# Local attention: values and sums in 64-key by 32-column tiles over 192 of 256 queries, in two turns with scores and the q, k projection between

## The chip, the core and the metric

The kernel runs on one core of a Trainium2 chip. A core has five engines that work side by side[...]: TensorE (PE in the profile; its weight loads are shown apart as PEld), VectorE (DVE), ScalarE (ACT), GpSimd (POOL), and SyncE (SP), which here only issues DMAs. PE writes its results into PSUM, a memory of eight banks; DVE and ACT read them from there[...]. The metric is the device time of one run in microseconds (us), lower is better; the times given are medians.

## The reference, cut to what matters

Two residual layers follow each other: `x = x + latent_attention(layernorm(x))`, then `x = x + ffn(layernorm(x))`, on x of 8 x 1024 x 256 in fp32. The "ffn" is itself a small transformer of two layers with local attention, and it is this part that the change touches. In it, per layer, with windows of 128 tokens, 8 heads and 64 dimensions a head:

```python
qkv = h @ wqkv
q = l2norm(q) * qs
k = l2norm(k) * ksc
q, k = rotary_xpos(q, k)
...
sim = jnp.einsum('bhwid,bhwjd->bhwij', bq, bk)        # a window's queries, its own and the previous window's keys
mask = (i < j) | (i > j + WINDOW) | (j == -1)
attn = jax.nn.softmax(jnp.where(mask, -big, sim), axis=-1)
out = jnp.einsum('bhwij,bhwjd->bhwid', attn, bv)
x = x + o @ wo
...
x = x + (a * gelu(g)) @ w2 + b2                       # the layer's MLP
```

A query sees keys of its own window up to itself, and of the window before from its own position on. Over one block of 128 keys, own and next window together, a key is therefore seen by at most 129 queries out of 256.

## The kernel before, in words

The kernel has two stages. `mla` does the latent attention for all eight sequences; `local` does the two layers of local attention and MLP. The change is in `local` alone.

`local` goes through 16 passes, one for each layer and sequence, and each pass through 8 windows: 128 steps in all, and then 11 more to finish. All work of the four compute engines in this loop is in an order written out by hand (`tc.manual_schedule`, L1026): each engine carries out its instructions in the order in which the loop emits them, and no engine takes one out of turn. A step does not work on one window from start to end; it takes one piece of several windows, so that results are ready long before they are read. In step s the kernel before emits, in this order (L1038 to L1052):

- `qk` of window s (L763): PE projects q and k into a tile of two PSUM banks. ACT squares it (L774), DVE multiplies with cosines and sines (L776, L779) and sums the squares by head (L784, L785), POOL computes the reciprocal norms (`rn`, L125), adds the two rope products (L788) and multiplies by the norms (L789).
- `transposes` of window s-2 (L802): q and k are turned on PE, in four transposes each, and ACT copies them out of PSUM as `qT` and `kT`.
- `v` of window s (L792): the projection of the values, copied out by ACT.
- one unit of the MLP.
- `values` of window s-4 (L847): PE multiplies the probabilities with the values (o) and with a column of ones (s, the sums), for four heads at a time, each head in 32 columns of the array and all 128 keys in its rows. A window has two blocks of keys, the one before and its own; the first window of a pass has one. DVE then takes the reciprocal of s and multiplies o with it (L869 to L878).
- `scores` of window s-3 (L813): for each half of the heads, sixteen matmuls on tiles of 64 rows by 32 columns over 160 queries. The scores are for the keys of this window against the queries of this and the next one, so the `qT` of window s-2 is needed. ACT takes the exponential (L834) and POOL sets to zero what a query must not see, in two `affine_select` instructions (L836 for the own window, L841 for the next one). The results are `pts`, two tiles for each window, read by `values` in the next step and once more in the one after that.
- every second step `output` (L882), the projection with `wo`, added by DVE and sent to DRAM.
- a second unit of the MLP.

The MLP works on chunks of 512 tokens, and each chunk is eight units (`mlp`, L927): five units with two up-projections each (`ag`, L945; one for the gate, which ACT turns through Gelu, L953, and one which DVE multiplies with it, L954), one with the single leftover up-projection (L958 to L967), and two with the down-projection (`psy`, L978), of which the second also turns the next chunk (L710). With two units a step, four steps are one chunk. The steps that end or begin a pass also turn the input of the next one (L737).

The PSUM pools (L585 to L588) hold two tiles of two banks, "pair", which `qk` and the two halves of `scores` use in turn; three buffers of one bank, "mm", for everything else on PE; and one bank for o. The sums s stand in an "mm" buffer. ACT loads a table before an exponential if the last one was for Gelu, and the other way round; these loads are at L834, L953 and L961.

Of the kernel before, what the change touches and what calls it, by code (L numbers as in the profile page):

```python
# [29 lines left out]
F32 = mybir.dt.float32  # L30
AF = mybir.ActivationFunctionType
ALU = mybir.AluOpType
AX = mybir.AxisListType
PSUM = bass.MemoryType.PSUM

P = 128
# [20 lines left out]
DEPTH, HEADS, DH, WINDOW = 2, 8, 64, 128  # L57
# [24 lines left out]
def preln_mla_local_kernel(  # L82
# [27 lines left out]
    nc = tc.nc  # L110
# [5 lines left out]
    ident = const.tile([P, P], F32, name="ident")  # L116
    make_identity(nc, ident)
    half = const.tile([P, 16], F32, name="half")
# [458 lines left out]
    def local(ctx: ExitStack, verdict):  # L577
# [4 lines left out]
        p1 = ctx.enter_context(tc.tile_pool(name="l1", bufs=1))  # L582
# [3 lines left out]
        psum = ctx.enter_context(tc.tile_pool(name="psum3", bufs=3, space=PSUM))  # L586
        ppair.append(ctx.enter_context(tc.tile_pool(name="pair1", bufs=1, space=PSUM)))
        pacc = ctx.enter_context(tc.tile_pool(name="pacc3", bufs=1, space=PSUM))  # L588
# [12 lines left out]
        ys = [dram.tile([T + 1, D], F32, tag=f"y{i}", name=f"y{i}") for i in range(3)]  # L601
        zero = p1.tile([1, P], F32, name="zero")
# [145 lines left out]
        class Pass:  # L748
# [53 lines left out]
            def transposes(self, i):  # L802
                key = self.key(i)
                self.kTs[i] = p1.tile([P, 4, P], F32, tag="kT", name=f"kT{key}", bufs=2)
                r = self.rot.pop(i)
                for n, dst in ((0, qT[:, :, i * P : (i + 1) * P]), (1, self.kTs[i])):
                    ps = psum.tile([P, 4, P], F32, tag="mm", name=f"psq{key}_{n}")
                    flat = r[:, n].rearrange("p h d -> p (h d)")
                    for c in range(4):
                        nc.tensor.transpose(ps[:, c, :], flat[:, c * P : (c + 1) * P], ident)  # L810
                    evac(dst, ps)

            def scores(self, i):  # L813

                n = 2 if i + 1 < NT else 1
                kT = self.kTs.pop(i)
                self.pts[i] = []
                for g in range(2):
                    key = f"{self.key(i)}_{g}"


                    flat = next(turns)
                    for c in range(2):
                        for j in range(2):
                            rows = slice(64 * j, 64 * j + DH)
                            for t in range(4):
                                keys = slice(32 * t, 32 * t + 32)
                                q0, q1 = 32 * t, min(32 * t + 32 + P, n * P)
                                nc.tensor.matmul(  # L829
                                    flat[keys, 2 * j + c, q0:q1], kT[rows, 2 * g + c, keys],  # L830
                                    qT[rows, 2 * g + c, i * P + q0 : i * P + q1], start=True, stop=True,
                                )
                    pt = p1.tile([P, 4, 2 * P], F32, tag="pt", name=f"pt{key}", bufs=5)
                    nc.scalar.activation(pt[:, :, : n * P], flat[:, :, : n * P], AF.Exp, scale=-1.0)  # L834

                    nc.gpsimd.affine_select(  # L836
                        out=pt[:, :, :P], in_=pt[:, :, :P], pattern=[[0, 4], [1, P]],
                        compare_op=ALU.is_ge, fill=0.0, base=0, channel_multiplier=-1,
                    )
                    if n == 2:  # L840
                        nc.gpsimd.affine_select(  # L841
                            out=pt[:, :, P:], in_=pt[:, :, P:], pattern=[[0, 4], [-1, P]],
                            compare_op=ALU.is_ge, fill=0.0, base=0, channel_multiplier=1,
                        )
                    self.pts[i].append(pt)

            def values(self, i):  # L847

                key, vs, pts, oTs = self.key(i), self.vs, self.pts, self.oTs
                blocks = [(i - 1, P)] if i else []  # L850
                blocks.append((i, 0))
                o = pacc.tile([P, 2, 2, P], F32, tag="acc", name=f"o{key}")
                s = psum.tile([P, 2, P], F32, tag="mm", name=f"s{key}")
                for g in range(2):
                    for a in range(3):
                        for m, off in blocks:
                            for j in range(4):
                                h = 4 * g + j
                                rows = slice(32 * j, 32 * j + 32)
                                if a < 2:  # L860
                                    left = vs[m][:, h * DH + a * 32 : h * DH + a * 32 + 32]
                                nc.tensor.matmul(  # L862
                                    o[rows, g, a, :] if a < 2 else s[rows, g, :],
                                    left if a < 2 else ones,
                                    pts[m][g][:, 2 * (j % 2) + j // 2, off : off + P],
                                    start=(m == blocks[0][0]), stop=(m == i),
                                )
                rs = p2.tile([P, 2, P], F32, tag="lrs", name=f"rs{key}")
                nc.vector.reciprocal(rs, s)  # L869
                if i % 2 == 0:  # L870
                    oTs[i // 2] = p2.tile([P, 4, 2 * P], F32, tag="oT", name=f"oT{key}")
                at = self.n * NT + i
                nc.vector.tensor_reduce(stats[:, 1, at : at + 1], s, AX.XY, ALU.add)
                nc.vector.tensor_tensor(
                    oTs[i // 2][:, :, (i % 2) * P : (i % 2 + 1) * P].rearrange("p (g a) q -> p g a q", g=2),
                    o, rs.unsqueeze(2).to_broadcast([P, 2, 2, P]), ALU.mult,
                )
                nc.vector.tensor_reduce(stats[:, 0, at : at + 1], rs, AX.XY, ALU.add)  # L878
                if i:
                    del vs[i - 1], pts[i - 1]  # L880
# [26 lines left out]
        made = {}  # L907
# [111 lines left out]
        def each(step, name, back):  # L1019
            j = step - back  # L1020
            if 0 <= j < windows:
                n, i = divmod(j, NT)
                getattr(made[n], name)(i)

        E = mybir.EngineType
        with tc.manual_schedule(engines={E.PE, E.DVE, E.Activation, E.Pool}):  # L1026
            for step in range(windows + LAG):
# [9 lines left out]
                if not late:  # L1037
                    each(step, "qk", 0)  # L1038
                each(step, "transposes", 2)
                if not late:  # L1040
                    each(step, "v", 0)
                if step >= LAG:
                    next(units, None)
                each(step, "values", 4)
                each(step, "scores", 3)
# [5 lines left out]
                if step >= LAG - 2:  # L1051
                    next(units, None)  # L1052
                if late:
                    each(step, "qk", 0)
                    each(step, "v", 0)
# [621 lines left out]
```

## Time and profile before

| | |
|---|---|
| median of 3 runs | 3622.2 us (3621.33 to 3624.78) |
| the profiled execution's own time | 3623.07 us |
| its span, first to last instruction | 3621.2 us |
| mean granted PE clock | 0.995 |
| PE busy | 3556.6 us (98%) |
| DVE, ACT, POOL busy | 2246.5, 1828.0, 1348.9 us |
| `local`: first qk to the last step's qk | about 1061 to 3482 us |

The profile is one execution. "Busy" is the time in which an engine had at least one instruction running; PE's matmuls overlap, so that a mean of 274 ns for one says little of what it costs in a row of them. Each fp32 matmul of the program stands in the trace as two matmul records, with two weight loads. An arrow "<-" after an idle time names what ended it.

### The profile page before, as it was taken

How to read it: one execution, taken by the hardware profiler on the slowest of the kernel's cores; microseconds unless marked ns; L12 is line 12 of the kernel's file. 1: busy time of each engine (PE TensorE's matmuls, PEld its weight loads, DVE VectorE, ACT ScalarE, POOL GpSimd, SP SyncE). 2: the span in 40 equal slices, each digit the busy share in tenths (PEclk: the TensorE clock that was granted, in tenths of full speed). 3: DMA queues.
4: the chain of work that ended last, by engine and by line, in shares of the span. 5: the costliest groups of instructions: out<-in, count | busy, mean ns of one | idle time of the engine just before them, and what ended most of it. 6: DMA issues, size and time to landing. Idle time of an engine off the chain costs nothing.

```text
span 3621.2 us, 77779 instructions
## 1 busy us (share of the span) xinstructions
PE 3556.6 (98%) x34338; PEld 2046.6 (57%) x34338; DVE 2246.5 (62%) x3273; ACT 1828.0 (50%) x2362; POOL 1348.9 (37%) x1031
## 2 busy tenths in 40 slices
PE   8999999999999999999999999999999999999999
PEld 3434443443345666666666666666666666666666
DVE  6888888888876545555555554555555555555543
ACT  5777777777653344444444444444444444444441
POOL 1001000100118545545454553545455454444530
PEclk9999999999999999999999999999999999999999
DMA  1000000000110000000010001111101110110011
GB/s 58 7 19 24 16 12 21 24 7 7 69 56 13 19 33 19 31 27 31 22 37 30 19 31 57 36 33 45 45 25 36 33 36 26 43 42 24 26 33 42
DMA packets 102838, 110.14 MB, mean 30 GB/s; under 512 B 12930, under 2 KB 87003, under 8 KB 102363
## 3 DMA queue, kind: packets, MB, share of 16 engines
q1 hardware_dynamic: 99354, 101.49, 8.8%
q8 instruction: 271, 4.44, 0.5%
q10 hardware_dynamic: 3136, 3.59, 0.3%
q14 instruction: 77, 0.62, 0.1%
HBM read 63.11 MB, written 41.94 MB: 29 GB/s over the span
## 4 chain that ended last, share of the span: by engine, by line
PE 90%; DVE 5%; ACT 3%; issue 1%; DMA 1%; POOL 0%; ACTq 0%; SPq 0%; DVEq 0%; POOLq 0%
PE ag L945 14%; PE pair L769 12%; PE psy L978 9%; PE sc L399 9%; PE acc L432 7%; PE psw L890 6%; PE o L862 6%; PE pv L796 6%; PE psq L810 3%; PE s L862 3%; PE pair L829 3%; DVE rs L869 2%; PE psq L183 2%; PE psR L183 2%; ACT pt L834 2%; PE psx L183 1%
## 5 line engine op out<-in xcount | busy, mean ns | idle before, releaser
L125 POOL TENSOR_TENSOR rn<-ss,half 128x16 f32<-128x16 f32 x128 | 372.1, 2907 | 1028.8 <-DVE ss L785 1028.8
L421 DVE TENSOR_TENSOR pt<-pt,er 128x1024 f32<-128x1024 f32 x576 | 678.3, 1224 | 6.9 <-ACT pt L407 6.7
L407 ACT ACTIVATE pt<-sc 128x1024 f32<-128x1024 f32 x576 | 558.9, 1023 | 244.1 <-PE sc L399 220.0
L945 PE MATMUL ag<-d,l 128*128 128x512 f32 x1408 | 641.3, 597 | 3.4 <-ACT qT L78 2.7
L769 PE MATMUL pair<-l_qkv,xT 128*128 128x512 f32 x1024 | 466.9, 599 | 3.7 <-ACT pt L834 2.0
L834 ACT ACT_TABLE_LOAD x120 | 154.0, 1283 | 620.4 <-PE pair L829 620.3
L945 PEld LDWEIGHTS ag<-d,l 128*128 128x128 f32 x1408 | 262.0, 190 | 311.7 <-issue 303.2
L776 DVE TENSOR_TENSOR t<-pair,l_cos 128x1024 f32<-128x1024 f32 x128 | 156.5, 1223 | 354.7 <-ACT sq L774 354.7
L399 PE MATMUL sc<-q,k 32*128 32x512 f32 (+3 forms) x3072 | 350.9, 524 | 7.4 <-ACT pt L407 7.0
L769 PEld LDWEIGHTS pair<-l_qkv,xT 128*128 128x128 f32 x1024 | 189.7, 191 | 237.6 <-issue 206.5
L869 DVE RECIPROCAL rs<-s 128x256 f32<-128x256 f32 x128 | 224.6, 1755 | 157.8 <-PE s L862 157.7
L954 DVE SCALAR_TENSOR_TENSOR hid<-ag,l_b,ge 128x512 f32<-128x512 f32 x160 | 120.2, 751 | 317.6 <-ACT ge L953 178.4
L380 POOL TENSOR_SCALAR_AFFINE_SELECT er<-er 128x128 f32<-128x128 f32 x64 | 62.7, 980 | 678.5 <-DVE least L378 678.5
L432 PE MATMUL acc<-pt,v 128*32 128x512 f32 (+3 forms) x3072 | 312.0, 500 | 1.9 <-DVE pt L421 1.9
L788 POOL TENSOR_TENSOR t<-t,t 128x1024 f32<-128x1024 f32 x128 | 306.4, 2394 | 0.0
L978 PE MATMUL psy<-l,hid 128*128 128x256 f32 x1280 | 297.1, 379 | 0.0
L774 ACT ACTIVATE sq<-pair 128x1024 f32<-128x1024 f32 x128 | 131.1, 1024 | 313.0 <-issue 218.8
L978 PEld LDWEIGHTS psy<-l,hid 128*128 128x128 f32 x1280 | 243.2, 190 | 46.7 <-issue 15.3
L862 PE MATMUL o<-pt,v 128*32 128x128 f32 x7680 | 260.1, 274 | 0.8 <-POOL pt L836 0.8
L862 PEld LDWEIGHTS o<-pt,v 128*32 128x32 f32 x7680 | 204.2, 110 | 85.7 <-issue 82.8
L834 ACT ACTIVATE pt<-pair 128x1024 f32<-128x1024 f32 (+1 forms) x256 | 234.7, 968 | 34.6 <-PE pair L829 33.3
L399 PEld LDWEIGHTS sc<-q,k 32*128 32x128 f32 x3072 | 141.0, 184 | 189.8 <-ACT pt L407 113.6
(132 smaller groups left out, 5188.4 us busy)
## 6 DMA issues: line engine op xcount, KB each, us to landing
y<-xs SPq DMA_DIRECT2D x128, 128.0 KB, 1.9
h<-y SPq DMA_DIRECT2D x32, 512.0 KB, 3.8
x<-in_L_attn_x_dram SPq DMA_DIRECT2D x16, 512.0 KB, 4.6
x2d<-x SPq DMA_DIRECT2D x32, 256.0 KB, 2.3
xs<-x2d SPq DMA_DIRECT2D x16, 512.0 KB
x<-x2d SPq DMA_DIRECT2D x16, 512.0 KB
xs<-xs SPq DMA_DIRECT2D x32, 256.0 KB, 2.6
xs<-xs SPq DMA_DIRECT2D x16, 512.0 KB, 5.4
```

Of the source, the lines that this page charges most:

```text
L125: nc.gpsimd.tensor_tensor(out_, in_, half[:, :n], ALU.pow)
L399: nc.tensor.matmul(two[n // 2][:, n % 2, lo : lo + w], self.k[g][rows, kb * P : (kb + 1) * P], self.q[rows, g // 2, q0 : q0 + w], start=Tr ...
L407: nc.scalar.activation(pt, sc, AF.Exp, scale=SCALE)
L421: nc.vector.tensor_tensor(t, t, er.to_broadcast([P, 1024 // w, w]), ALU.mult)
L432: nc.tensor.matmul(self.acc[g][32 * n : 32 * n + 32, q0 - c * 512 :], self.v[:, kb, h * VW : h * VW + 32], pts[n // 2][:, n % 2, lo : lo + w],
L769: nc.tensor.matmul(qk[:, n].rearrange("p h d -> p (h d)"), self.left(i)[c], w["qkv"][:, c, n * INNER : (n + 1) * INNER], start=(c == 0), s ...
L788: nc.gpsimd.tensor_tensor(t1, t1, t2, ALU.add)
L834: nc.scalar.activation(pt[:, :, : n * P], flat[:, :, : n * P], AF.Exp, scale=-1.0)
L862: nc.tensor.matmul(o[rows, g, a, :] if a < 2 else s[rows, g, :], left if a < 2 else ones, pts[m][g][:, 2 * (j % 2) + j // 2, off : off + P ...
L869: nc.vector.reciprocal(rs, s)
L945: nc.tensor.matmul(ps, w["1"][:, c, i, :], d[:, c, :], start=(c == 0), stop=(c == 1))
L978: nc.tensor.matmul(ps[:, t, :], left, w["2"][:, i, :], start=(i == 0), stop=(i == NF))
```

## The change

It has five parts.

- **Tiles of values.** The keys of a block are cut in two halves of 64. A matmul of `values` now has 64 rows by 32 columns, so that eight instead of four run side by side, and each half of a block is only multiplied for the queries that can see it: 128 for one half and 64 for the other. The sums are one more part of the same tile, which grows to two banks; the two halves of rows write to different banks (`g = half ^ turn`).
- **Two turns.** In turn 0 the first half of keys does heads 0 to 3 and the second half heads 4 to 7; turn 1 is the other way round. After turn 1 comes the division.
- **Order of the step.** It is now: transposes of q, values turn 0, scores half 0, transposes of k, qk, scores half 1, values turn 1, v, a unit, output, a unit. In steps without qk a unit stands in its place, and near the end one unit moves ahead.
- **Buffers.** "mm" has two buffers instead of three.
- **Table switches.** A one-element Gelu follows scores half 1 on ACT, and a one-element exponential ends the step; each brings the load of its table to that place.

```diff
-        psum = ctx.enter_context(tc.tile_pool(name="psum3", bufs=3, space=PSUM))
+        psum = ctx.enter_context(tc.tile_pool(name="psum3", bufs=2, space=PSUM))
...
+        spot = p1.tile([1, 2], F32, name="spot")
+        nc.gpsimd.memset(spot, 0.0)
...
-            def values(self, i):
-                key, vs, pts, oTs = self.key(i), self.vs, self.pts, self.oTs
-                blocks = [(i - 1, P)] if i else []
-                blocks.append((i, 0))
-                o = pacc.tile([P, 2, 2, P], F32, tag="acc", name=f"o{key}")
-                s = psum.tile([P, 2, P], F32, tag="mm", name=f"s{key}")
-                for g in range(2):
-                    for a in range(3):
-                        for m, off in blocks:
-                            for j in range(4):
-                                h = 4 * g + j
-                                rows = slice(32 * j, 32 * j + 32)
-                                if a < 2:
-                                    left = vs[m][:, h * DH + a * 32 : h * DH + a * 32 + 32]
-                                nc.tensor.matmul(
-                                    o[rows, g, a, :] if a < 2 else s[rows, g, :],
-                                    left if a < 2 else ones,
-                                    pts[m][g][:, 2 * (j % 2) + j // 2, off : off + P],
-                                    start=(m == blocks[0][0]), stop=(m == i),
-                                )
+            def values(self, i, turn):
+                vs, pts = self.vs, self.pts
+                if turn == 0:
+                    self.o = pacc.tile([P, 2, 4, P], F32, tag="acc", name=f"o{self.key(i)}")
+                own = [(i, 0, 0, P), (i, 0, P // 2 if i else 0, P)]
+                before = [(i - 1, P, 0, P // 2), (i - 1, P, 0, P)]
+                blocks = [own[:1] + before[:1], before[1:] + own[1:]] if i else [own[:1], own[1:]]
+                last = len(blocks[0]) - 1
+                for a in range(3):
+                    for n in range(last + 1):
+                        for j in range(4):
+                            for half in range(2):
+                                m, off, q0, q1 = blocks[half][n]
+                                g = half ^ turn
+                                h = 4 * g + j
+                                keys = slice(64 * half, 64 * half + 64)
+                                left = vs[m][keys, h * DH + a * 32 :][:, :32] if a < 2 else ones[keys]
+                                nc.tensor.matmul(
+                                    self.o[32 * j : 32 * j + 32, g, a, q0:q1], left,
+                                    pts[m][g][keys, 2 * (j % 2) + j // 2, off + q0 : off + q1],
+                                    start=(turn == a == n == 0), stop=(turn == 1 and a == 2 and n == last),
+                                )
+                if turn == 1:
+                    self.divide(i)
...
-                if not late:
+                attend = step < windows and not late
+                end = windows + 2 <= step < windows + 4
+                each(step, "transposes", 2, 0)
+                each(step, "values", 4, 0)
+                each(step, "scores", 3, 0)
+                each(step, "transposes", 2, 1)
+                if attend:
                     each(step, "qk", 0)
-                each(step, "transposes", 2)
-                if not late:
+                else:
+                    for _ in range(1 + end):
+                        next(units, None)
+                each(step, "scores", 3, 1)
+                nc.scalar.activation(spot[:, 1:], spot[:, :1], AF.Gelu)
+                each(step, "values", 4, 1)
+                if attend:
                     each(step, "v", 0)
-                if step >= LAG:
-                    next(units, None)
-                each(step, "values", 4)
-                each(step, "scores", 3)
+                    if step >= LAG:
+                        next(units, None)
...
-                if step >= LAG - 2:
+                if step >= LAG - 2 and not end:
                     next(units, None)
+                nc.scalar.activation(spot[:, 1:], spot[:, :1], AF.Exp)
```

`transposes` and `scores` do what they did, now for one of their two halves at a call; `divide` holds the lines that ended `values`, with s read from the third part of o.

## The prediction

> **What bounds the kernel now.** I read the page first, for the busy shares, the forty slices and the costliest groups:
>
> ```profile
> PE 3556.6 (98%) x34338; PEld 2046.6 (57%) x34338; DVE 2246.5 (62%) x3273; ACT 1828.0 (50%) x2362; POOL 1348.9 (37%) x1031
> ...
> POOL 1001000100118545545454553545455454444530
> ...
> L862 PE MATMUL o<-pt,v 128*32 128x128 f32 x7680 | 260.1, 274 | 0.8 <-POOL pt L836 0.8
> ```
>
> PE is busy throughout; from slice 12 on (about 1060 us, where the local attention begins) POOL is at about half. The values' matmuls lose 0.8 us in all to POOL's masks: that wait is hidden today, and it is the one I follow. Next, the groups kept apart by shape, for 1300 to 3560 us: name, count, then busy us and mean ns.
>
> ```profile
> L862 PE MATMUL o<-pt,v 128*32 128x128 f32 x6912 | 233.6, 274 | 0.0
> ...
> L862 PE MATMUL s<-pt,ones_l 128*32 128x128 f32 x3456 | 136.5, 273 | 0.0
> L829 PE MATMUL pair<-qT,kT 64*32 64x160 f32 x6359 | 131.2, 299 | 0.0
> ```
>
> Values and sums take 370 us of PE in that stretch; a saving has to come from there. Then the timeline of one step (columns: start us, length us, engine, line, what):
>
> ```profile
> 2416.36 3.60 PE L769 MATMUL pair<-l_qkv,xT 128*128 128x512 f32 x8
> 2419.79 1.04 PE L810 MATMUL psq<-ident,t 128*128 128x128 f32 x8
> 2420.04 1.02 ACT L774 ACTIVATE sq<-pair 128x1024 f32<-128x1024 f32 x1 [3.17 <-issue]
> ...
> 2421.10 1.23 DVE L776 TENSOR_TENSOR t<-pair,l_cos 128x1024 f32<-128x1024 f32 x1 [3.44 <-ACT sq L774]
> ...
> 2424.68 0.17 DVE L785 TENSOR_SCALAR ss<-ss 128x16 f32<-128x16 f32 x1
> 2424.94 2.91 POOL L125 TENSOR_TENSOR rn<-ss,half 128x16 f32<-128x16 f32 x1 [10.98 <-DVE ss L785]
> 2425.91 1.08 PE L862 MATMUL o<-pt,v 128*32 128x128 f32 x32
> ...
> 2427.81 2.37 POOL L788 TENSOR_TENSOR t<-t,t 128x1024 f32<-128x1024 f32 x1
> ...
> 2428.67 1.32 PE L829 MATMUL pair<-qT,kT 64*32 64x160 f32 x64
> ...
> 2430.26 1.90 POOL L789 TENSOR_TENSOR t<-t,rn 128x1024 f32<-128x1024 f32 x1
> ...
> 2432.11 0.63 POOL L836 TENSOR_SCALAR_AFFINE_SELECT pt<-pt 128x512 f32<-128x512 f32 x1
> ```
>
> PE ends qk at 2419.79; POOL ends that window's rope multiply at 2432.16, 12.37 us later, and only then masks the scores. Across the steps this 12.37 is the median and nearly the minimum. It costs nothing now: the masks' reader, values, comes in the next step, at about 2443.4. Last, busy time by stretch (PE, then the other engines), on the grid on which the granted clock changes (PEclk, third number from the end):
>
> ```profile
> 1074.53:1077.94 3.41, 1.35 (x7) 0.53 (x7) 2.47 (x4) 0.00 (x0) 2.77 (x2) 1.00 0.00 0
> 1077.94:1081.36 3.42, 3.42 (x10) 1.87 (x9) 1.35 (x2) 1.99 (x3) 3.22 (x2) 0.50 0.00 0
> ```
>
> A stretch of 3.41 us with PE mostly idle is followed by one at half clock.
>
> **The skill.** TensorE: Matmul & The Clock Gate, section "Architectural detail": the queues of ScalarE, VectorE and GpSimd are strict FIFO. The trace agrees: a mask never passes the rope multiply ahead of it. The same page, Part 1: the clock is halved after an idle window of about 3.4 us; the two rows above agree. TensorEngine Tiling (Array Packing), "Key Properties": tiles work independently, and changing the mode drains the array. The trace agrees: the eight 64x32 tiles of scores start 7 ns apart and every eight take 0.136 us (160 columns); the four 128x32 tiles of values take 0.109 us (128 columns); around each change of mode about 0.09 us is empty.
>
> **The saving.** Now a window with two blocks has 96 records, 24 fours x 0.109 = 2.62 us. After it, a turn has for each of three parts two eights of 128 columns and two of 64: 3 x (2 x 0.109 + 2 x 0.055) = 0.98 us, both turns 1.97. No 64-column eight is in the trace; 0.055 is half of 0.109 and also eight starts of 7 ns. At worst it costs the full 0.109 (2.62, nothing saved). I take 0.055: 0.65 us saved per window, nothing in the first window of each pass (no block before). Mode changes go from three to four a step: +0.09. Net -0.56 us where PE sets the pace; 16 passes x (7 x 0.65 - 8 x 0.09) = 61 us at most.
>
> **The moved mask.** A step is now: q transposes, values turn 0, scores half 0, k transposes, qk, scores half 1, values turn 1, v, units. POOL's order, as built, is: masks of half 0, rn, add, multiply (all of this step's qk), masks of half 1. The next step's values turn 0 reads half 1 after its first eights (0.22 us), and everything on PE queues behind it: scores, transposes, the next qk. From the end of qk to that mask's end: 12.37 + 0.64 = 13.0 us, with PE's wake of 0.05 (its start after a mask at 1124.39). PE's work in that time: mode change 0.09, half the scores 0.54, values 0.98, change 0.09, v 1.72, units U, transposes 0.44, change 0.09, first eights 0.22: 4.2 + U. From release to the next qk's end: 0.76 + 0.54 + 0.09 + 0.44 + 3.43 = 5.26. So no step is shorter than 13.0 + 5.26 = 18.27 us. An up unit is 3.43. U is 6.9 in a step with two (A), 10.3 with an output too (B), 5.1 with one and the leftover chunk (C), over 14 with two down units (D). A lacks 1.9, C 3.7 us; B and D are covered.
>
> **The table switches and the third buffer.** The Exp dummy sits after the last unit; the next ACT item is the q copy, for which scores half 0 wait. The switch is 1.28 us (row of L834 loads). In A and C the mask is later still, so this is free; without the mask C would pay some 1.5. In D it is paid: with two buffers in place of three the chunk's second group of transposes waits for the adding of psy (0.2 + 0.69 + 0.05, less the 0.44 of the first group): +0.5; then evacuation 0.77, switch 1.28, dummy (not in the trace, 0.1 to 0.3; 0.2 taken), copy 0.58: scores start 1.55 late. Together 2.05 us. In the D of a pass that also turns the next stream, the same waits push its transposes: 2.75. The two switches each step replace those at L834 and L953; ACT at 50% hides them elsewhere. One memset: nothing.
>
> **Sum.** Qk to qk, the steps of a pass now repeat as D 24.81, A 17.10, B 19.24, C 15.61, D 26.11, A 19.02, B 20.55, C 15.61 = 158.05 us, 14 times from 1241.6 to 3482 us (one odd step at the layer change, left as it is). After: 26.3, 18.27, 19.0, 18.27, 28.3, 18.27, 20.0, 18.27 = 166.7: +8.65, x14 = 121. The three steps before: +2.6. The seven steps from the first scores to the first chunk's units (1081.8 to 1169.9 us: 88.1 us, 12.6 each) have little PE work and become 7 x 18.27 = 127.9: +39.8. Together +163. The clock: in C PE now idles 3.4 us on end, and in this trace every stretch of the grid with at most 1.54 us of PE busy was followed by half clock (six before the end), those with 1.73 and 1.82 were not; by where the grid falls that is about 8 cases in 10, each losing half of most of a 3.41 us window in the path to the next qk: 1.2 x 29 = 35; the seven idle steps at the start 10. Both from 0 to twice that. Tail and the join to the first stage: 0, +-5. 3621.2 + 208 = 3829 span; around it lie 1.9 us (3623.07), and the median 3622.2 stands 0.9 under that run. Forecast 3830 us.
>
> **Rivals.** *The clock holds.* The mask binds, but the half clock is not granted, as gaps are broken by small matmuls: 3622 + 163 = 3785. For it: the price rests on six stretches of this trace. *The mask is hidden (faster).* If the masks of half 1 are ready within 9.3 us of qk's end, PE's work in C, nothing waits and the tiles' 61 us are gained: 3561; with D's waits of 4.8 us a pass still there, about 3630. Against: 12.37 us is the sum of seven measured instructions on queues that keep order. The turning point is 9.3 us for C and 11.0 for A. *The halves don't overlap.* If the two row halves run one after the other, a turn costs 1.97: +0.8 in A and C, +2 in B and D, some 165 us more: 3990. Against: scores run so already. *It cancels:* 3622.
>
> **Chances.** Mask and clock 0.55, mask alone 0.26, mask hidden and faster 0.07, D's waits alone (3630, just slower) 0.04, no overlap 0.05, cancels 0.03. A difference under 0.2% (7 us) can't be told here. Faster 0.07, same 0.04, slower 0.89. The range holds the two mask cases with their unknowns: 3740 (163 less 45) to 3890 (clock at twice its price, 0.3 us more per wait).
>
> **What would show it.** PE's values waiting for POOL's mask, about 1.9 us in A and 3.7 in C, POOL never idle between the multiply and that mask; steps of 18.3 us or more in place of 15.6; scores waiting for the q copy after D; granted clock under 0.99; PE's busy share near 92%. Wrong if masks of half 1 start before the multiply ends, or if C stays under 17 us.

## The result, and the profile after

The changed kernel takes 3906.7 us (median of 4 runs, 3903.89 to 3908.08) against 3623.4 us before: ratio 1.0782, 95% interval 1.0765 to 1.0799. It is slower by 283 us, where I had forecast 208 slower; 3906.7 lies 17 us above the upper end of my range. The profiled execution has a span of 3905.2 us against 3621.2, and a mean granted clock of 0.977 against 0.995.

The page of the kernel after: busy time by engine, POOL and the granted clock in forty slices, and the costliest group of the new matmuls (busy us, mean ns | idle of PE ahead of them, and what ended it).

```profile
PE 3643.8 (93%) x45858; PEld 2096.4 (54%) x45858; DVE 2223.0 (57%) x3273; ACT 1947.5 (50%) x2683; POOL 1355.2 (35%) x1032
...
POOL 1000100010154544445444544444444444444440
PEclk9999999999978999999999999999999999999999
...
L876 PE MATMUL o<-pt,v 64*32 64x128 f32 (+1 forms) x15360 | 274.4, 254 | 149.4 <-POOL pt L843 138.2 <-DVE oT L895 11.1
```

PE falls from 98% to 93%. The wait that was 0.8 us before, values for POOL's mask, is 138.2 us. Slices 12 and 13 are the first local attention windows, where the clock is granted least. The waits of PE by kind (us in total, how many, longest):

```profile
PE o L876 <- POOL pt L843: 138.2, 52, 9.4
PE pair L836 <- ACT qT L78: 21.5, 17, 4.7
PE psq L814 <- ACT xT L78: 19.9, 15, 1.3
PE o L876 <- DVE oT L895: 11.1, 4, 3.8
PE psth L712 <- DVE xs L998: 10.8, 31, 0.3
```

The second and third are waits for the copies that stand behind Exp's table. The last is the missing third buffer: it isn't among the waits of the kernel below that gets this buffer back. The groups of values kept apart by shape, for 1300 to 3700 us (busy us, mean ns):

```profile
L876 PE MATMUL o<-pt,v 64*32 64x128 f32 x7104 | 207.6, 278 | 17.4 <-POOL pt L843 17.4
...
L876 PE MATMUL o<-pt,v 64*32 64x64 f32 x6240 | 164.4, 220 | 81.0 <-POOL pt L843 81.0
L876 PE MATMUL o<-pt,ones_l 64*32 64x128 f32 x3552 | 147.0, 285 | 0.3 <-issue 0.3
```

Before, values alone were 233.6 us busy in such a stretch; now the two shapes are 372.0. Busy time of groups that overlap can't be added, but there is no saving to be seen here. Last, one step C in the timeline (start, length, engine, line):

```profile
2521.23 2.91 POOL L125 TENSOR_TENSOR rn<-ss,half 128x16 f32<-128x16 f32 x1 [6.61 <-DVE ss L787]
...
2524.11 2.35 POOL L790 TENSOR_TENSOR t<-t,t 128x1024 f32<-128x1024 f32 x1
...
2525.69 0.51 PE L876 MATMUL o<-pt,v 64*32 64x128 f32 x18
...
2526.55 1.90 POOL L791 TENSOR_TENSOR t<-t,rn 128x1024 f32<-128x1024 f32 x1
...
2528.40 0.64 POOL L843 TENSOR_SCALAR_AFFINE_SELECT pt<-pt 128x512 f32<-128x512 f32 x1
...
2529.09 0.65 PE L876 MATMUL o<-pt,v 64*32 64x64 f32 x42 [2.89 <-POOL pt L843]
...
2529.87 0.32 PE L836 MATMUL pair<-qT,kT 64*32 64x160 f32 x1
2529.87 0.33 PE L876 MATMUL o<-pt,ones_l 64*32 64x64 f32 x11
2529.99 0.30 PE L836 MATMUL pair<-qT,kT 64*32 64x160 f32 x1
2530.00 0.23 PE L876 MATMUL o<-pt,ones_l 64*32 64x64 f32 x2
...
2532.08 4.44 PE L771 MATMUL pair<-l_qkv,xT 128*128 128x512 f32 x8
```

(Half 0 and half 1 are the probabilities of heads 0 to 3 and 4 to 7.) Turn 0 runs its first 18 records, which read this window's half 0 and what the window before left, and stops at the first that reads this window's half 1. POOL doesn't pause from rn to that half's mask. PE stands for 2.89 us, and the next qk takes 4.44 us where the row of before had 3.60. The same place on the grid of the clock (PE, PEld, DVE, ACT and POOL busy, then the granted clock):

```profile
2526.95:2530.36 3.41, 1.27 (x98) 1.27 (x105) 2.52 (x9) 1.18 (x3) 3.30 (x4) 1.00 0.00 0
2530.36:2533.77 3.41, 3.41 (x34) 1.90 (x17) 0.00 (x0) 1.58 (x2) 1.61 (x3) 0.50 0.02 5
```

### The profile page after: what moved, and what is told of

It is laid out like the page before. It is cut to its first block, busy times and chain, and to the rows that moved or that the text cites. A ratio compares the mean times of both kernels' runs of the same rounds, so it can differ in the third digit from the quotient of the medians.

```text
span 3905.2 us, 101096 instructions
## 1 busy us (share of the span) xinstructions
PE 3643.8 (93%) x45858; PEld 2096.4 (54%) x45858; DVE 2223.0 (57%) x3273; ACT 1947.5 (50%) x2683; POOL 1355.2 (35%) x1032
## 5 line engine op out<-in xcount | busy, mean ns | idle before, releaser
L964 PE MATMUL ag<-d,l 128*128 128x512 f32 x1408 | 626.7, 593 | 0.7 <-ACT ge L972 0.7
L771 PE MATMUL pair<-l_qkv,xT 128*128 128x512 f32 x1024 | 478.9, 611 | 0.0
L841 ACT ACTIVATE pt<-pair 128x1024 f32<-128x1024 f32 (+1 forms) x256 | 248.2, 970 | 388.0 <-PE pair L836 144.4
L876 PE MATMUL o<-pt,v 64*32 64x128 f32 (+1 forms) x15360 | 274.4, 254 | 149.4 <-POOL pt L843 138.2
L843 POOL TENSOR_SCALAR_AFFINE_SELECT pt<-pt 128x512 f32<-128x512 f32 x256 | 164.1, 641 | 605.8 <-ACT pt L841 605.8
L876 PEld LDWEIGHTS o<-pt,v 64*32 64x32 f32 x15360 | 234.2, 107 | 183.5 <-POOL pt L843 148.6
L972 ACT ACTIVATE ge<-ag,l_b 128x512 f32<-128x512 f32 x160 | 109.9, 687 | 343.0 <-PE ag L964 342.2
L716 ACT ACTIVATE d<-psth,l_s,l_g 128x512 f32<-128x512 f32 x64 | 49.8, 778 | 421.7 <-PE psth L712 421.6
L798 PE MATMUL pv<-l_qkv,xT 128*128 128x512 f32 x512 | 253.6, 618 | 0.0
```

Of the source, the lines that this page charges most:

```text
L771: nc.tensor.matmul(qk[:, n].rearrange("p h d -> p (h d)"), self.left(i)[c], w["qkv"][:, c, n * INNER : (n + 1) * INNER], start=(c == 0), s ...
L798: nc.tensor.matmul(pv, self.left(i)[c], self.w["qkv"][:, c, 2 * INNER :], start=(c == 0), stop=(c == 1))
L876: nc.tensor.matmul(self.o[32 * j : 32 * j + 32, g, a, q0:q1], left, pts[m][g][keys, 2 * (j % 2) + j // 2, off + q0 : off + q1], start=(tur ...
L964: nc.tensor.matmul(ps, w["1"][:, c, i, :], d[:, c, :], start=(c == 0), stop=(c == 1))
```

## The experiments

All times below are medians of 4 runs. Steps are read from qk to qk in the trace and given as means over the passes, without the odd step at the change of layer. D', A' and B2 are the longer D, A and B of the forecast's list, D, A and B1 the shorter:

```
                            D'     A'     B2     C      D      A      B1     C      pass
before                      26.03  19.02  20.55  15.61  24.85  17.10  19.24  15.59  158.0
forecast, without clock     28.3   18.27  20.0   18.27  26.3   18.27  19.0   18.27  166.7
after                       29.09  18.85  20.68  19.00  27.11  18.27  20.15  19.50  172.7
rope after the masks        29.04  19.29  20.72  15.64  26.68  16.83  20.25  16.74  165.2
and Exp's table later       27.30  19.16  20.71  15.65  25.74  16.99  20.24  15.51  161.3
best guess                  26.61  18.68  21.00  15.70  25.44  17.28  20.12  15.84  160.7
```

**POOL's order.** In the changed kernel, rn, add and multiply are taken out of qk as a method of their own and given to POOL after the scores of half 1, and so after its masks.

```diff
                 each(step, "scores", 3, 1)
+                if attend:
+                    each(step, "rope", 0)
```

> The changed kernel, but on POOL rn, add and multiply of qk are put behind both masks of half 1; the orders of PE, ACT and DVE are untouched and every instruction is kept. If half 1's masks behind POOL's long run are what stretches steps A, C and the start steps, waits of values for POOL's masks fall from 138 us to under 40 us and the time to about 3750 us (3735 to 3785), that is 120 to 170 us below the changed kernel. If the steps are long for another reason (the turns of values themselves, the table switches, the buffers), the time stays above 3880 us. Third possibility: the transposes of the second next step now wait for the later multiply, and part of the gain comes back as waits of psq for POOL.

3748.6 us (1.0346 of before, 1.0329 to 1.0364): 158 us off, with every instruction kept. The timeline of this kernel in a step before a D (start, length, engine, line) and its group of values on the page:

```profile
2460.35 0.63 POOL L847 TENSOR_SCALAR_AFFINE_SELECT pt<-pt 128x512 f32<-128x512 f32 x1 [4.65 <-ACT pt L845]
...
2460.94 0.63 POOL L852 TENSOR_SCALAR_AFFINE_SELECT pt<-pt 128x512 f32<-128x512 f32 x1
...
2462.25 2.91 POOL L125 TENSOR_TENSOR rn<-ss,half 128x16 f32<-128x16 f32 x1 [0.68 <-DVE ss L787]
```

```profile
L880 PE MATMUL o<-pt,v 64*32 64x128 f32 (+1 forms) x15360 | 258.6, 252 | 11.1 <-DVE oT L899 11.1
```

The masks now run ahead of rn, and no wait for POOL is left in front of values. A falls from 18.27 to 16.83, the Cs from 19.0 and 19.5 to 15.6 and 16.7; the granted clock is 0.992. The third possibility, the transposes waiting for the multiply, didn't come: they wait 8.7 us once, as in the changed kernel. The waits of scores for q's copy grow to 37.7 us in 33: what the mask had covered in C.

**The order with the old tiles.** The changed order, turns and buffers, with 128-row tiles: all 128 keys and 256 queries in 24 matmuls, one half (g) a turn.

```diff
-                vs, pts = self.vs, self.pts
+                vs, pts, g = self.vs, self.pts, turn
...
-                            for half in range(2):
-                                m, off, q0, q1 = blocks[half][n]
-                                g = half ^ turn
-                                h = 4 * g + j
-                                keys = slice(64 * half, 64 * half + 64)
+                            h = 4 * g + j
```

> The changed kernel's order, turns and buffers, but with 128-row by 32-column tiles of values as before (one g a turn, all keys and queries, 24 matmuls a turn). If 64-column eights had the forecast's price (0.055 us, 0.65 us a window), this is 73 us slower than the changed kernel, about 3980 us. If a turn of 48 short matmuls takes as long as one of 24 long ones, as the trace of the changed kernel reads (1.29 us a turn against 1.31), this is within 15 us of the changed kernel: 3892 to 3922 us. If it is faster than the changed kernel by over 15 us, the short tiles cost more than they save.

3773.4 us, 133 below the changed kernel. For "over 15 us faster" I had written that the short tiles cost more than they save, and that doesn't follow: I had overlooked that this edit does two things. With 128-row tiles turn 0 reads half 0 alone, and half 1 is read in turn 1, many microseconds later; with 64-key tiles turn 0 must read both halves, since the two row halves of one turn work on different heads. The next kernel takes this apart: the same tiles, dealt out so that turn 0 starts with half 1.

```diff
-                for a in range(3):
+                for g, a in ([(1, 0), (0, 0), (0, 2)], [(0, 1), (1, 1), (1, 2)])[turn]:
```

> The order alone (128-row tiles in the changed kernel's order) came out at 3773 us, 133 below the changed kernel. There turn 0 takes half 0's probabilities alone; with the small tiles turn 0 takes both halves, because keys 64 to 127 of one turn belong to the other half's heads. This kernel is the order alone, with the 24 matmuls dealt out anew so that turn 0 begins with half 1's probabilities (o columns 0 to 31 of both halves and half 0's sums first, the rest in turn 1): same tiles, same count, same durations. If it is the need of half 1's mask in turn 0, the loss comes back whole: 3905 to 3945 us (the changed kernel and up to 0.3 us a window for the old tiles), with 110 to 150 us of waits of values for POOL. If the small tiles themselves stretched the changed kernel's steps, it stays at 3765 to 3790 us.

3952.3 us, 179 more than with one half a turn, and 7 above the band I gave. The waits of PE in this kernel:

```profile
PE o L865 <- POOL pt L843: 138.8, 52, 9.7
PE pair L836 <- ACT qT L78: 19.9, 17, 4.1
```

The same 52 waits, the same 138 us, without one small tile in the kernel. So the loss belongs to the need of half 1's mask in turn 0 together with POOL's order. It also prices the tiles, as dealt out, within this order: 3952.3 - 3906.7 = 46 us in their favour. Not all of it is the tile: the changed kernel has 18 records of turn 0 ahead of the wait, this kernel none.

**A dose.** One more mask (half 0's own keys again) on POOL between the multiply and half 1's masks of the changed kernel.

```diff
+                if g == 1:
+                    first = self.pts[i][0]
+                    nc.gpsimd.affine_select(out=first[:, :, :P], in_=first[:, :, :P], ...)
```

> The changed kernel with one more POOL instruction of about 0.65 us, half 0's first mask once more, between POOL's multiply and the masks of half 1. If POOL's run from qk to half 1's mask sets steps A, C and the start steps, each step in which values wait becomes longer by the added 0.65 us: 52 such waits, so 33 to 45 us more, 3940 to 3955 us, and the waits of values for POOL grow from 138 us by about as much. If POOL has slack and something else sets these steps, the time stays within 8 us of 3907.

3954.2 us: 47 more for one mask in each window, 0.59 us of POOL from start to start.

```profile
PE o L882 <- POOL pt L845: 162.4, 51, 9.7
```

The added mask writes half 0, which turn 0 reads first, so the waits now end with it and not with half 1's own mask, and their sum can't be held against the 138 us as it stands. (One more wait, of 9.0 us, is listed under DVE ves L694, though PE starts 0.05 us after the added mask there too.) The steps are the better measure: where the clock held, A goes from 18.27 to 18.85 us and C from 18.4 to 19.0, which is the added 0.59. The granted clock falls to 0.970, and longer steps at half clock are the rest as far as I can see. POOL has no slack in these steps.

**The tile alone.** Two kernels keep before's order but for one thing: turn 0 stands between qk and the transposes, turn 1 where values stood (and near the end one unit moves ahead, as in the change). Both have two product buffers and two banks for o, as the change does. First with old tiles, then with new ones.

```diff
                     each(step, "qk", 0)
+                each(step, "values", 4, 0)
                 each(step, "transposes", 2)
...
-                each(step, "values", 4)
+                each(step, "values", 4, 1)
```

> The kernel before with its order of every other thing, 128-row tiles, but two PSUM buffers in place of three, two banks for o, and the values of half 0 moved ahead of the transposes (half 1 stays). It is the control for the next one. Expected 3640 to 3720 us: qk to values of half 0 may wait for a mask in the short steps (15.61 us), and the units wait for one buffer less. If it is as slow as the changed kernel (over 3850 us), the two buffers or the early turn do the damage, not POOL's order.

> The same as the two turns with old tiles, but with the 64-key by 32-column tiles over 192 of 256 queries: the tile alone, POOL's order as before. With the forecast's price of 0.055 us for a 64-column eight, 73 us below its control; if 48 short matmuls take as long as 24 long ones, within 15 us of it. Above it by more than 15 us: the short tiles cost more than the old ones. Either way it should stay under 3750 us, since half 1's masks are not behind rn, add and multiply here; over 3850 us would mean that the tiles do the damage.

3757.8 us with old tiles, above the 3640 to 3720 that I expected, and 3747.1 with new ones: the tile saves 10.7 us in 112 windows, 0.10 us each, not 0.65. Both stay far below the changed kernel, and neither waits long for a mask (6.6 and 12.7 us in all). Then the new tiles over all 256 queries:

```diff
-                own = [(i, 0, 0, P), (i, 0, P // 2 if i else 0, P)]
-                before = [(i - 1, P, 0, P // 2), (i - 1, P, 0, P)]
+                own = [(i, 0, 0, P), (i, 0, 0, P)]
+                before = [(i - 1, P, 0, P), (i - 1, P, 0, P)]
```

> The two turns with new tiles (3747.1 us), but over all 256 queries: the 64-column matmuls have 128 columns, counts and order are the same. With the forecast's prices (0.055 us an eight against 0.109) it is 73 us slower, 3820 us. If an eight of 64 columns costs what one of 128 does, as the changed kernel's trace reads, it is within 10 us: 3737 to 3757 us. In between would mean that the supply of matmuls and their columns share the time.

And with 16 columns in place of 64, which leaves out 48 queries, so that their sums are not complete:

```diff
-                own = [(i, 0, 0, P), (i, 0, P // 2 if i else 0, P)]
-                before = [(i - 1, P, 0, P // 2), (i - 1, P, 0, P)]
+                own = [(i, 0, 0, P), (i, 0, P - 16 if i else 0, P)]
+                before = [(i - 1, P, 0, 16), (i - 1, P, 0, P)]
```

> The two turns with new tiles (3747.1 us), where each 64-column matmul of values and sums is cut to 16 columns: 48 of its queries are left out, so those sums are not complete; count, order and everything else stay. From the starts of the matmuls, a turn up to the k or q transposes behind it takes 1.52 us with 128 columns in the second six eights and 1.40 us with 64, where the columns alone would have made it 0.33 us shorter. If the array's columns set a turn, the six eights lose another 6 x 0.041 = 0.25 us: 1.15 us, and with two turns in 112 windows 55 us: about 3692 us. If from 64 columns on the supply of 48 matmuls (about 27 ns each) sets it, only the last eight ends sooner: 1.34 to 1.40 us, 3733 to 3750 us.

3767.3 us with 128 columns, 3747.1 with 64, 3742.2 with 16. Cutting half of six eights gives 20 us, where my price gave 73; cutting three quarters of the rest gives 5. Turn 0 in these kernels, from its first matmul to the first transpose behind it, and the part of it after the last matmul's start, by the starts of PE's records (us, medians):

```
columns in six of the 12 eights     turn to transpose    last start to transpose    first to last start
128                                 1.524                0.200                      1.324
 64                                 1.400                0.147                      1.253
 16                                 1.335                0.110                      1.225
old tiles, 24 matmuls               1.448                0.203                      1.245
```

From 128 to 64 columns, the last eight leaves the array 0.053 us sooner, which is my 0.055, and from 64 to 16 another 0.037 (48 columns, 0.041 by the same rate). But below 128 columns the stretch from first to last start hardly moves: 1.253 and 1.225 us for 48 matmuls, some 26 ns each. Single starts show why. The first two short eights of a turn still keep the array's pace: each takes 0.109 us with 128 columns, 0.056 with 64 and 0.040 with 16. From the 32nd record on, the starts come at 14.5, 14.2 and 14.2 ns a record (means over the rest of the turn), whatever their columns; with 128 columns the array itself needs 13.6 (0.109 for eight). So the array's own time of a short eight was priced right; after the first thirty records it isn't what sets a turn.

The Trainium skill, TensorEngine Tiling (Array Packing), "Instruction Overhead", says that each matmul has an overhead of about 60 cycles and warns against taking a tiling factor from a dimension that is small already. With the full clock of 2.4 GHz that TensorE: Matmul & The Clock Gate states in Part 1, that is an estimate of 25 ns, 1.20 us for 48. The runs agree in size only if the overhead falls once on a matmul of the program: each is two records, which come 13 to 14 ns apart. Whether it is this overhead, or the weight load that each record has, they don't show. I had read the page for its tiles and left this out.

**Two buffers.** The kernel before, values undivided, with the change's PSUM budget.

```diff
-        psum = ctx.enter_context(tc.tile_pool(name="psum3", bufs=3, space=PSUM))
+        psum = ctx.enter_context(tc.tile_pool(name="psum3", bufs=2, space=PSUM))
...
-                o = pacc.tile([P, 2, 2, P], F32, tag="acc", name=f"o{key}")
-                s = psum.tile([P, 2, P], F32, tag="mm", name=f"s{key}")
+                self.o = pacc.tile([P, 2, 4, P], F32, tag="acc", name=f"o{self.key(i)}")
```

> The kernel before with its tiles and its order, with nothing but the PSUM budget of the change: two buffers for products instead of three, and o with its sums in two banks. From the steps of the two turns with old tiles against before (D +1.35, D' +1.80, A' +1.57, all others +0.79) I read 0.79 us a step for parting the turns and for a product that waits for a copy, and 0.56, 1.0 and 0.78 a pass for the buffers: 3645 to 3680 us. If the buffers are the larger cause of the 134 us that the two turns with old tiles lose, 3720 us or more; if the third buffer was worth nothing, 3615 to 3635 us.

3783.1 us, 158 above before, and over 100 above what I had read from the steps. Its waits of PE:

```profile
PE pv L796 <- ACT qT L78: 94.9, 124, 0.8
PE psts L710 <- ACT ge L954: 17.7, 14, 1.3
PE psth L710 <- DVE xs L980: 10.4, 30, 0.3
```

In before's order v's product follows the transposes of q and k at once; with two buffers it must take q's and waits 0.77 us for its copy, 124 times. With what PE loses around such a stop, a step is 1.0 us longer (C 16.63 us in place of 15.61), which is most of the 158. I had read the buffers off the D steps alone. In the kernels above, turn 0 ahead of the transposes covers part of it (29.9 us left), which is why these are quicker than this one. In the changed order v's product stands elsewhere, so the buffer was tried there too: the order with old tiles (3773.4 us), o in one bank, the sums in turn 1 out of three product buffers.

```diff
-                    self.o = pacc.tile([P, 2, 4, P], F32, tag="acc", name=f"o{self.key(i)}")
+                    self.o = pacc.tile([P, 2, 2, P], F32, tag="acc", name=f"o{self.key(i)}")
+                else:
+                    self.s = psum.tile([P, 2, P], F32, tag="mm", name=f"s{self.key(i)}")
...
-                for a in range(3):
+                for g, a in ([(0, 0), (0, 1)], [(1, 0), (1, 1), (0, 2), (1, 2)])[turn]:
```

> The order alone with old tiles (3773 us), with the third PSUM buffer back: o keeps one bank, the sums come from the product buffers and are formed in turn 1, which has 32 matmuls, turn 0 has 16. In the order of before two buffers cost 158 us, 0.77 us of it in every step as a wait of v's product for the copy of q. In the changed order v's product doesn't follow the transposes, so I expect the third buffer to matter only in D and D' (waits of the layer norm's transposes, 0.5 us each): 10 to 35 us off, 3738 to 3763 us. If two buffers cost the changed order as much as the old one, 3620 us.

3749.8 us: 24 off, as expected. The same buffer is worth 158 us in one order and 24 in the other. But the 24 is what is left of more. The waits of scores for q's copy, with two buffers and then with three:

```profile
PE pair L836 <- ACT qT L78: 37.0, 33, 3.6
PE pair L836 <- ACT qT L78: 71.9, 47, 4.6
```

Part of what the buffer frees is lost again in front of the copy that stands behind Exp's table. This kernel also has 16 matmuls in turn 0 and 32 in turn 1, so it isn't the buffer alone.

**Exp's table.** The kernel with the rope after the masks (3748.6 us), with the activation that fetches Exp's table moved from the end of a step to behind the copy of q at the start of the next.

```diff
                 each(step, "transposes", 2, 0)
+                nc.scalar.activation(spot[:, 1:], spot[:, :1], AF.Exp)
...
-                nc.scalar.activation(spot[:, 1:], spot[:, :1], AF.Exp)
```

> The changed kernel with rn, add and multiply put behind the masks of half 1 (3748.6 us), and with the activation that fetches Exp's table put behind the copies of q in place of ahead of them, at the end of the step. In steps D the scores then don't wait for a copy of q that stands behind the table (1.09 us in 33 of them) nor the transposes of q for a copy behind it (1.49 us in 13). Theory: 30 to 50 us off, 3700 to 3720 us, with these two waits under 15 us together. If the table only moves in front of the Exp that scores of half 1 wait for, or what waited for q's copy next waits for a mask, under 15 us is won: 3735 to 3750 us.

3688.0 us: 61 off, more than the 30 to 50 expected. Scores wait 4.7 us for q's copy in place of 37.7, and psq for the copy of xT is gone from the list (21.2 before): 54 us. By the steps: D' -1.7, D -0.9, and the C before D' -1.2. Without either of the two fetching activations:

```diff
-                nc.scalar.activation(spot[:, 1:], spot[:, :1], AF.Exp)
-                nc.scalar.activation(spot[:, 1:], spot[:, :1], AF.Gelu)
```

> The kernel with Exp's table fetched behind the copy of q (3688 us), without either of the two activations that fetch a table ahead of need. The tables change as often as before, but in the first Exp of half 0 and in the first Gelu of a unit. If the two activations cost only what they take (0.20 us each) and hide nothing, 3670 to 3690 us. If they hide a table, then without them Gelu comes 1.3 us late where a unit follows, and with two product buffers the matmuls of the unit wait for it: 3720 to 3800 us.

3688.2 us, the same. They hide nothing that counts; only a fetch in a wrong place costs.

**The best guess.** Old tiles, three product buffers, Exp's table behind q's copy, all in the changed order.

> The third buffer with old tiles in the changed order, and Exp's table fetched behind the copy of q: everything that was found to cost time is taken out, apart from the order itself. From 3773 less about 60 for the table and 10 to 35 for the buffer: 3675 to 3705 us. If it comes under 3620 us, the changed order is better than the old one once it has its buffer; if not, what is left over before, 50 to 85 us, belongs to the order (one mode change of the array more in each step, the slower start).

3678.4 us (1.0150 of before, 1.0132 to 1.0168), 71 less than with the table where it was. For the local attention's passes, 1260 to 3540 us, the view of PE's waits names one, at the change of layer:

```profile
PE pair L836 <- ACT qT L78: 4.7, 1, 4.7
```

What is left is the order itself. The first D' comes 18.7 us later than before (1260.3 against 1241.6 us), and a pass is 2.7 us longer, 0.34 a step. In this kernel PE goes into a mode of tiles twice a step where before it went once, and changes between values and scores twice. By the starts of the records, going in costs 0.093 us (0.522 from a 512-column product to values, 0.429 to another product), changing from scores to values 0.137 (0.226 against 0.089 inside a group), and going out to v's product 0.113 (0.202 against 0.089) and another 0.104 before its second record. One of each, less 0.05 because the transposes that now follow the scores lose less than a unit did, is 0.40 us a step. The order also takes away a wait of 0.83 us a pass, 0.10 a step: that leaves 0.30 of the 0.34. With the new tiles values and scores share a mode, and scores start 0.010 us after values; the changed kernel spends only the going in and out. No kernel tried is under before's 3623, and nothing measured here points to one: the tiles' best saving was 46 us, and they take the bank of the third buffer.

## Why the prediction was wrong, step by step

**The moved mask: right.** Named signs came: waits for POOL's mask, POOL without a pause, no step of a regular pass under 18.27. A is 18.27 in the trace: 12.80 us from the end of qk to the end of the mask, 0.05 to PE's start, 1.89 to the next qk and 3.53 for it. The forecast had 13.0, 1.83 and 3.43, so the mechanism is right and the agreement to the hundredth is luck. C is 18.4 where the clock held. PE waits 1.3 us in A and 2.9 in C, not 1.9 and 3.7: it comes to the wait later than forecast. Taking away its cause gave 158 us back, the clock's loss among them.

**The saving: this is the step that failed.** It priced a turn at 0.98 us from "0.055 is half of 0.109 and also eight starts of 7 ns" and took 0.65 us off each window. A turn takes 1.29 us up to the change of mode (1.386 to v's product, less 0.093): 1.240 from first to last start and 0.053 for the last eight. The array's time for a short eight was right; what failed is that PE would go on starting eight records in 0.055 us, which holds for the first two short eights of a turn alone. Turn and scores together are 2.03 + 1.95 us a window in the changed kernel against 4.005 before. With the second entry into the mode (0.09) and the slower first transpose behind it (0.06) that is 0.12 us more than before, where I had -0.56. B2 shows it clean: 20.55 + 0.12 = 20.67; measured 20.68, forecast 20.0. My own upper bound, "at worst it costs the full 0.109", was the value to take.

In the steps that PE paces, the forecast is short by 1.15 (B1), 0.7 (B2), 0.6 (A') and 0.8 each (D, D'): 4.0 us a pass, 56 in 14. The saving that didn't come is 0.68 in each of A', B2, D and D', 2.7 together. B1 holds a slip in the sum besides. Before does the values of a pass's first window (one block, 48 records) whole in B1. The changed order does their turn 0 already in A, and in B1 their turn 1 and the next window's turn 0: the trace has 144 records of values and sums in A and in B1. At the forecast's own prices these are 6 x 0.109 + 0.98 = 1.64 us in B1 against 1.31 before, so B1 comes to 19.24 + 0.33 + 0.09 = 19.66, not 19.0; the other 0.5 is the price of a turn again. A' too comes to 18.46 by the forecast's working (19.02 - 0.56), not 18.27; it ended lower than the turns' price would put it because a wait of 0.83 us before is 0.48 now. About 0.1 in D and in D' stays open. The Cs came out 0.5 a pass under the forecast with its clock, and the odd step at the change of layer, left as it was, 7 us over; these cancel.

**The start: too small.** I had 18.27 us for each of seven steps, and 10 for the clock. The trace has 19.9 to 20.8 each, at a mean clock of 0.79 from 1062 to 1200 us. With the join and the steps up to the first D' (1315.6 against 1241.6 us), 74 us against my 52: 22 more. Some 6 of them lie in the seven steps, 6 in the four steps behind them, and 10 ahead of them (the first of the seven begins at 1092.1 us, before at 1081.8), where I had put nothing.

**The clock: about right in C, as a mean.** 1.2 us a step C gives 19.5; measured 19.0 and 19.5. By the mean clock, 90 us of full speed are lost in the span (0.023 of 3905) against 18 before. The limit that I had read from before, 1.54 us of PE busy in a stretch of the grid, isn't one. In the changed kernel the clock held after stretches with 1.51 and 1.55 us and fell after two with 1.78 and 1.79:

```profile
1745.34:1748.75 3.41, 1.51 (x110) 1.35 (x110) 2.31 (x8) 0.94 (x3) 3.30 (x4) 1.00 0.00 0
1748.75:1752.17 3.42, 3.42 (x13) 1.83 (x12) 0.00 (x0) 1.07 (x2) 0.78 (x2) 1.00 0.02 5
...
2202.70:2206.10 3.40, 1.78 (x49) 1.38 (x54) 0.00 (x0) 3.10 (x6) 0.00 (x0) 1.00 0.08 30
2206.10:2209.50 3.40, 3.40 (x103) 2.91 (x98) 0.00 (x0) 0.86 (x2) 0.00 (x0) 0.50 0.02 5
```

**The table switches and the third buffer: right in kind.** "Without the mask C would pay some 1.5": one of the two Cs paid 1.2. Scores wait 0.93 us after D, not 1.55. The buffer's 0.5 in D and 1.2 in D' make 24 us in 14 passes, and 24 were measured in this order, but by luck: with the buffer back D went from 26.84 to 26.94 us and D' from 29.8 to 28.0, while the waits for q's copy grew by 35 us. What it would cost elsewhere I couldn't have read from D.

**The sum.** 208 forecast, 56 for the steady steps, 22 for the start, and 2 less at the end (137.0 us after the last qk, 139.1 before) make 284; the spans differ by 284.0.

**The rivals.** "The clock holds" fell with 37 stretches at half clock, 7 before; "the mask is hidden" with the 138 us. "The halves don't overlap" would have had turns of 1.97 us; they take 1.29.

## What to carry to other kernels

A tile that halves the columns halved the array's time here, not the time of a turn: price short matmuls by their count too, and if a bound says "nothing saved", ask which measurement rules it out before taking the other end. When a product is dealt out anew, list what each part must have ready: here the pairing of key halves with heads pulled half 1's mask into the earlier turn, and an in-order POOL behind it cost more than the tile could bring. A buffer's worth depends on what stands next to it in the order; measure it in the order that will be used.

## What the runs showed that I had not expected

- 48 matmuls of 64 keys by 32 columns need 1.225 to 1.253 us from first to last start with 16 or 64 columns in half of them, 1.324 with 128 in all.
- From the 32nd record of a turn on, the starts come about 14 ns apart with 16, 64 or 128 columns in half of them; only the first two short eights keep the array's pace.
- The third product buffer is worth 158 us in before's order and 24 us in the changed one, where Exp's table takes part of it back.
- Fetching Gelu's and Exp's tables ahead of need made no difference (3688.0 and 3688.2 us), but Exp's fetch ahead of q's copy cost 61 us.
- The change from 128-row values to 64-row scores takes 0.203 us from the last start, 0.010 when both are 64-row tiles.
- On 64-row tiles PE doesn't start everything in the order in which it was emitted: in the step C shown, the first scores start ahead of 13 records of sums that stand before them in the program. For PE's tiles, "no engine takes one out of turn" doesn't hold by these starts.
